# Sums and lower parts of the second layer's weight blocks on GpSimd instead of VectorE

## Chip, cores and metric

The kernel runs on one core of a Trainium2 chip. The metric is the device time of one execution in microseconds, taken as the median of the runs. Besides TensorE (PE in the profile) a core has VectorE (DVE), ScalarE (ACT), GpSimd (POOL) and SyncE (SP), each with an instruction queue of its own that is worked off in order. Nearly all transfers are issued from SP's queue.

## The reference, cut to what matters

Four batches of 512 rows and 256 columns go through two layers. Each layer normalizes the rows, computes a mixer (a recurrence with one step in the first layer, causal attention in the second) and a gated feed-forward block of width 1024 with a Walsh-Hadamard transform, and adds the product of mixer and gate to the input:

```python
xn = _layernorm(x, axis=-1)
s = _L1_attn_ref(xn, L1_attn_qkv, L1_attn_o_proj, L1_attn_gamma, L1_attn_beta)
g = _silu(_L1_ffn_ref(xn, L1_ffn_W1, L1_ffn_W2, L1_ffn_W3))
x = x + s * g

def _L1_ffn_ref(x, W1, W2, W3):
    up_gate = jnp.einsum('bsd,hd->bsh', x, W1)
    up_lin = jnp.einsum('bsd,hd->bsh', x, W3)
    hidden = jax.nn.silu(up_gate) * up_lin
    hidden = fwht(hidden)
    return jnp.einsum('bsh,dh->bsd', hidden, W2)
```

Everything is float32.

## The kernel before

**Products in two parts.** TensorE multiplies in a rounded float32 format (`F32R`). To keep float32 accuracy an operand is split into an upper part, the value rounded, and a lower part, the value minus the upper part. `split` (L59) does this: a cast on ScalarE (L61) and a subtraction on VectorE (L62). A product is three matmuls: upper by upper, upper by lower, lower by upper (`mm3`, L80). Every matmul of the kernel is recorded at L70, every split at L61 and L62, so the profile is read by tile names rather than lines.

**First layer.** `ffn` (L474) runs once per batch. For each of eight chunks `c` it makes two products of 128x512 (`f_<b>gu<c>`, three PSUM banks in turn), a silu on ScalarE (L535), the gate product on VectorE (L537, which frees the second bank), the split of the hidden tile (`f_<b>hh`, `f_<b>hl`), and, one chunk later, 24 down products of 128x256 into `f_<b>dn`.

**Work beside it.** `Beside` (L893) deals out other tasks between the chunks: the gate of the batch before (L714, L716), the mixer (L725, with `osb`, the scale `ssr` and its power on GpSimd at L740), and the norm of the next batch (`norm`, L438), which ends in a power on GpSimd (L282), the normalization (L284), and eight transposes on TensorE. The first products of a batch need the split result of these transposes, `xt`.

**The second layer's weights.** The second layer computes a 2x2 block product with seven products instead of eight; for that it needs, besides blocks of the weights, four sums of blocks. `prep_s(q)` (L327) makes them for block pair `q` of four: it loads four blocks (`sraw`, 512 KB), forms the sums `ssum` (L335 to L338, where L337 reads L335's result and L338 L337's), splits three of the blocks (128x768, after which the parts are called `sp`) and the four sums (128x1024), and stores the parts to DRAM (`s`, L347). It runs for pair 0 in the third batch of the first layer (batch 2) ahead of the next batch's norm, for pairs 1 and 2 later in that batch's tasks, and for pair 3 in batch 3. `load_s` (L350) loads the parts (`sw`, 896 KB each) for every pair of every batch of the second layer, into buffers that the first layer's weights leave. Raw blocks, sums, parts, and many other tiles share ten buffers of the tag `t4` in turn.

**Order.** In the first layer a scheduler arranges the instructions of each engine's queue from the order and the dependencies of the program; `after(...)` forces single pairs. In the second layer TensorE's order is written out by hand (`line["fixed"]`, L1089).

GpSimd runs, apart from five memsets, only the small powers at L266, L282, L402 and L740.

Of the kernel before, what the change touches and what calls it, by code (L numbers as in the profile page):

```python
# [17 lines left out]
ALU = mybir.AluOpType  # L18
# [17 lines left out]
def kernel(ctx: ExitStack, tc: tile.TileContext, a: dict, out: bass.AP):  # L36
    nc = tc.nc
# [6 lines left out]
    def t4(name, shape, dt=F32):  # L44
        return act.tile(shape, dt, tag="t4", name=name, bufs=10)
# [13 lines left out]
    def split(src, hi, lo, engine=nc.vector):  # L59

        h = nc.scalar.copy(hi, src)  # L61
        return h, engine.tensor_tensor(lo, src, hi.bitcast(F32), ALU.subtract)  # L62
# [264 lines left out]
    def prep_s(q):  # L327

        raw = t4(f"sraw{q}", [P, 4, D])
        nc.sync.dma_start(raw, a["w13_1"][q])  # L330
        yield
        sums = t4(f"ssum{q}", [P, 4, D])
        a11, a12, a22, a21 = (raw[:, i, :] for i in range(4))
        s1, s2, s3, s4 = (sums[:, i, :] for i in range(4))
        nc.vector.tensor_tensor(s1, a21, a22, ALU.add)  # L335
        nc.vector.tensor_tensor(s3, a11, a21, ALU.subtract)
        nc.vector.tensor_tensor(s2, s1, a11, ALU.subtract)  # L337
        nc.vector.tensor_tensor(s4, a12, s2, ALU.subtract)  # L338
        yield
        sdram[q] = there = [  # L340
            dram.tile([P, 7, D], F32, tag=f"s{i}", name=f"s{i}_{q}", bufs=4) for i in range(2)
        ]
        for at, n, src in ((0, 3, raw), (3, 4, sums)):
            parts = [t4(f"sp{at}_{i}_{q}", [P, n, D], F32R) for i in range(2)]
            split(src[:, :n, :], *parts)
            for i in range(2):
                nc.sync.dma_start(there[i][:, at : at + n, :], parts[i].bitcast(F32))  # L347
            yield
# [573 lines left out]
    def run(f, *args):  # L922
        return lambda: f(*args)
# [90 lines left out]
    for b in range(B):  # L1014
# [8 lines left out]
        if b + 1 < B:  # L1023
            if b:
                load_x(b + 1)
            if b == 2:
                tasks.append((prep_s(0), 4))
            tasks.append((norm(0, b + 1), NORM))
# [11 lines left out]
        if b == 2:  # L1040
            tasks += [(prep_s(1), 4), (norm(1, 0), NORM), (prep_s(2), 4)]
        if b == 3:
            atts = [Attention(0)]
            at = atts[0]
            parts = run(at.xt_half, 0), run(at.xt_half, 1), at.xt, at.scaled, at.split_sums
            tasks += [(call(f), 1) for f in parts]
            norms = {1: norm(1, 1)}
            tasks.append((prep_s(3), 4))
# [158 lines left out]
```

## Time and profile before

| what | value |
|---|---|
| median of three runs (lowest, highest) | 358.3 us (358.22, 358.42) |
| span of the profiled execution | 356.7 us |
| mean granted TensorE clock in it | 0.998 |
| VectorE busy | 287.2 us, 598 instructions |
| ScalarE busy | 197.8 us, 374 instructions |
| GpSimd busy | 20.8 us, 22 instructions |
| HBM read, written | 42.40 MB, 9.45 MB |

The span runs from the first to the last instruction of the profiled execution; the device time of a run also holds what lies around it. That execution has no device time of its own beside its span; the median is 1.6 us above the span. In the profile's lines a name such as `f_2hl<-f_2h,f_2hh` gives the tile written and the tiles read, with buffer numbers left out; in lists of groups come the count, the busy time and the mean duration of one, in a timeline the start, the duration and, in square brackets, the idle time before and what ended it. Busy time of TensorE is modelled at its ends: matmuls overlap, so a 128x512 matmul is shown with some 0.39 us though the next starts 0.23 us later.

### The profile page before, as it was taken

To read this page: it belongs to the slowest core of one execution; us is meant where nothing else is said; L and a number is where in the kernel's file an instruction comes from. 1 tells how busy PE (TensorE), PEld (TensorE's weight loads), DVE (VectorE), ACT (ScalarE), POOL (GpSimd) and SP (SyncE) were. 2 spreads that over 40 slices of the span, in tenths; PEclk is the share of its full clock that TensorE was granted. 3 is DMA by queue.
4 is the path that set the end of the run, shared out by engine and by line. 5 is a ranking of instruction groups with operands and counts; after the bars stand their busy time and mean duration, and the time that the engine had idled before them with its cause. 6 is when DMAs were issued, how large, how long until landed. Compare 5 with 4: busy or idle time off the path is not lost.

```text
span 356.7 us, 6276 instructions
## 1 busy us (share of the span) xinstructions
PE 350.9 (98%) x2477; PEld 327.5 (92%) x2477; DVE 287.2 (81%) x598; ACT 197.8 (55%) x374; POOL 20.8 (6%) x22
## 2 busy tenths in 40 slices
PE   8999999999999999999999999999999999999995
PEld 6878998888988898888999999999999999999994
DVE  6899659998579938998887957989679897678646
ACT  3666166265463425674467655586555676556443
POOL 2000110300020210100110001100011000000000
PEclk9999999999999999999999999999999999999999
DMA  6935000301044317656257145662554635445401
GB/s 208 367 98 205 2 1 2 117 0 61 0 167 163 145 38 230 257 174 191 118 208 265 36 172 209 217 201 115 206 187 168 230 158 206 143 152 186 199 2 59
DMA packets 16284, 52.25 MB, mean 146 GB/s; under 512 B 1632, under 2 KB 7936, under 8 KB 16256
## 3 DMA queue, kind: packets, MB, share of 16 engines
q1 hardware_dynamic: 15968, 51.60, 40.8%
q8 instruction: 19, 0.31, 0.4%
q10 hardware_dynamic: 288, 0.26, 0.2%
q14 instruction: 9, 0.07, 0.1%
HBM read 42.40 MB, written 9.45 MB: 145 GB/s over the span
## 4 chain that ended last, share of the span: by engine, by line
PE 98%; DVE 1%; ACT 0%; issue 0%
PE f_0dn L70 6%; PE f_1dn L70 6%; PE f_2dn L70 6%; PE f_0gu L70 6%; PE f_1gu L70 6%; PE f_2gu L70 6%; PE f_3gu L70 6%; PE f_3dn L70 6%; PE sc L70 4%; PE pv L70 4%; PE o L70 3%; PE v L70 3%; PE tq L70 3%; PE warm L70 2%; PE w2ps L70 1%; PE pt L70 1%
## 5 line engine op out<-in xcount | busy, mean ns | idle before, releaser
L70 PE MATMUL f_3gu<-xt,w 128*128 128x512 f32 x96 | 25.0, 396 | 0.0
L70 PE MATMUL f_2gu<-xt,w 128*128 128x512 f32 x96 | 24.8, 395 | 0.0
L70 PE MATMUL f_1gu<-xt,w 128*128 128x512 f32 x96 | 24.8, 395 | 0.0
L70 PE MATMUL f_0gu<-xt,w 128*128 128x512 f32 (+1 forms) x108 | 24.3, 378 | 0.0
L70 PEld LDWEIGHTS f_0gu<-xt,w 128*128 128x128 f32 x108 | 18.4, 188 | 4.5 <-issue 0.7
L70 PEld LDWEIGHTS f_1gu<-xt,w 128*128 128x128 f32 x96 | 17.0, 188 | 3.1
L70 PEld LDWEIGHTS f_2gu<-xt,w 128*128 128x128 f32 x96 | 17.0, 188 | 3.0
L70 PEld LDWEIGHTS f_3gu<-xt,w 128*128 128x128 f32 x96 | 17.0, 188 | 2.9
L61 ACT CAST f_2hh<-f_2h 128x512 fp32r<-128x512 f32 x16 | 10.0, 623 | 15.6 <-DVE f_2h L537 12.4
L70 PE MATMUL f_3dn<-w2l,f_3hh 128*128 128x256 f32 x64 | 17.7, 281 | 0.0
L70 PE MATMUL f_3dn<-w2h,f_3hh 128*128 128x256 f32 x64 | 17.7, 281 | 0.0
L70 PE MATMUL f_1dn<-w2l,f_1hh 128*128 128x256 f32 x64 | 17.7, 281 | 0.0
L70 PE MATMUL f_2dn<-w2h,f_2hh 128*128 128x256 f32 x64 | 17.7, 282 | 0.0
L70 PE MATMUL f_1dn<-w2h,f_1hh 128*128 128x256 f32 x64 | 17.6, 280 | 0.0
L70 PE MATMUL f_2dn<-w2l,f_2hh 128*128 128x256 f32 x64 | 17.6, 280 | 0.0
L70 PE MATMUL f_3dn<-w2h,f_3hl 128*128 128x256 f32 x64 | 17.0, 281 | 0.0
L70 PE MATMUL f_1dn<-w2h,f_1hl 128*128 128x256 f32 x64 | 17.0, 281 | 0.0
L70 PE MATMUL f_2dn<-w2h,f_2hl 128*128 128x256 f32 x64 | 16.7, 281 | 0.0
L61 ACT CAST f_3hh<-f_3h 128x512 fp32r<-128x512 f32 (+1 forms) x17 | 10.0, 595 | 10.2 <-DVE f_3h L537 6.0
L61 ACT CAST f_1hh<-f_1h 128x512 fp32r<-128x512 f32 x16 | 9.9, 621 | 9.7 <-DVE f_1h L537 6.6
L62 DVE TENSOR_TENSOR f_2hl<-f_2h,f_2hh 128x512 fp32r<-128x512 f32 x16 | 10.9, 684 | 4.5 <-ACT f_2hh L61 4.5
L62 DVE TENSOR_TENSOR f_3hl<-f_3h,f_3hh 128x512 fp32r<-128x512 f32 (+1 forms) x17 | 11.1, 655 | 3.7 <-ACT f_3hh L61 3.6
(487 smaller groups left out, 1147.7 us busy)
## 6 DMA issues: line engine op xcount, KB each, us to landing
sw<-s SPq DMA_DIRECT2D x32, 896.0 KB, 5.9
s<-sp SPq DMA_DIRECT2D x8, 512.0 KB, 4.2
s<-sp SPq DMA_DIRECT2D x8, 384.0 KB, 2.8
w2raw<-in_w SPq DMA_DIRECT2D x4, 512.0 KB, 5.5
sraw<-in_w SPq DMA_DIRECT2D x4, 512.0 KB, 3.5
mrb<-there SPq DMA_DIRECT2D x4, 512.0 KB, 3.8
w13raw<-in_w SPq DMA_DIRECT2D x3, 512.0 KB, 7.2
x<-in_x SPq DMA_DIRECT2D x3, 512.0 KB, 3.4
```

The source lines that it names most:

```text
L61: h = nc.scalar.copy(hi, src)
L62: return h, engine.tensor_tensor(lo, src, hi.bitcast(F32), ALU.subtract)
L70: ins = call(*args, **kwargs)
```

## The change

The four sums of `prep_s` and the subtractions of its two splits are issued on GpSimd. The casts stay on ScalarE, the transfers on SP. It applies to all four block pairs. `split` already has a parameter for the engine of the subtraction, with VectorE as the default.

```diff
         sums = t4(f"ssum{q}", [P, 4, D])
         a11, a12, a22, a21 = (raw[:, i, :] for i in range(4))
         s1, s2, s3, s4 = (sums[:, i, :] for i in range(4))
-        nc.vector.tensor_tensor(s1, a21, a22, ALU.add)
-        nc.vector.tensor_tensor(s3, a11, a21, ALU.subtract)
-        nc.vector.tensor_tensor(s2, s1, a11, ALU.subtract)
-        nc.vector.tensor_tensor(s4, a12, s2, ALU.subtract)
+        nc.gpsimd.tensor_tensor(s1, a21, a22, ALU.add)
+        nc.gpsimd.tensor_tensor(s3, a11, a21, ALU.subtract)
+        nc.gpsimd.tensor_tensor(s2, s1, a11, ALU.subtract)
+        nc.gpsimd.tensor_tensor(s4, a12, s2, ALU.subtract)
         yield
...
         for at, n, src in ((0, 3, raw), (3, 4, sums)):
             parts = [t4(f"sp{at}_{i}_{q}", [P, n, D], F32R) for i in range(2)]
-            split(src[:, :n, :], *parts)
+            split(src[:, :n, :], *parts, engine=nc.gpsimd)
             for i in range(2):
                 nc.sync.dma_start(there[i][:, at : at + n, :], parts[i].bitcast(F32))
             yield
```

Line numbers are the same in both kernels. The scheduler arranges the queues anew. In the built order of the changed kernel:

- GpSimd: pair 0's L335 to L337 and 768-column subtraction stand ahead of mixer 2's power (L740); L338 and the 1024-column subtraction follow it. Pair 1's sums and 768-column subtraction stand ahead of the two powers at L282 of batch 2 (batch 3's norm and the second layer's first norm), its last subtraction after them. Pair 2 stands ahead of mixer 3's power, and pair 3, without its last subtraction, ahead of the power of the second layer's batch 1.
- SP: the load of pair 1 stands, as before, after the stores of pair 0's first three parts; of these the store of the cast sums is now the last, where it was the store of the 768-column lower part. The load of pair 3 stands after one more weight load (`sw`, pair 1).
- TensorE: the same instructions; some groups of products change places, among them the eight transposes for batch 3, which stand after twelve more down products of batch 2.

## Prediction

> **What bounds the kernel now.** I read the page first (busy shares, the chain that ended last), then what TensorE waited for, then busy time by stretch, then the timelines of VectorE, GpSimd and TensorE between 95 and 175 us, where the change lies.
>
> ```profile
> PE 350.9 (98%) x2477; PEld 327.5 (92%) x2477; DVE 287.2 (81%) x598; ACT 197.8 (55%) x374; POOL 20.8 (6%) x22
> ...
> PE 98%; DVE 1%; ACT 0%; issue 0%
> ```
>
> TensorE is busy 98% of the span and is 98% of the chain. Its whole list of waits is one line:
>
> ```profile
> PE warm L70 <- DVE zr L941: 1.5, 1, 1.5
> ```
>
> So TensorE waits once, for the first tile at the start. The stretches confirm it (length, then busy us of PE, weight loads, DVE, ACT, POOL, with instruction counts; clock; DMA share; GB/s):
>
> ```profile
> 104.00:112.00 8.00, 8.00 (x44) 6.84 (x43) 7.70 (x19) 2.56 (x4) 1.48 (x1) 1.00 0.78 262
> 112.00:120.00 8.00, 8.00 (x48) 6.90 (x47) 8.00 (x27) 3.18 (x5) 2.55 (x2) 1.00 0.34 132
> ...
> 136.00:144.00 8.00, 8.00 (x50) 7.05 (x49) 7.04 (x13) 4.46 (x9) 0.00 (x0) 1.00 0.70 231
> ...
> 152.00:160.00 8.00, 8.00 (x44) 6.79 (x44) 8.00 (x13) 6.14 (x10) 0.00 (x0) 1.00 0.51 152
> ```
>
> TensorE is full in each, at granted clock 1.00. VectorE is full in two of them but nobody on the chain waits for it. Work taken off VectorE can therefore shorten nothing; the question is only whether something arrives late enough to open a hole in TensorE.
>
> **What is removed.** The rows of the moved work, four of each (ns min/median/max, first and last start):
>
> ```profile
> L335 DVE TENSOR_TENSOR ssum<-sraw x4: 415/418/426, 98.4 to 158.3; 128x256 f32<-128x256 f32 x4
> L338 DVE TENSOR_TENSOR ssum<-sraw,ssum x4: 412/421/426, 99.6 to 162.0; 128x256 f32<-128x256 f32 x4
> L62 DVE TENSOR_TENSOR sp<-sraw,sp x4: 917/952/953, 102.5 to 159.0; 128x768 fp32r<-128x768 f32 x4
> L62 DVE TENSOR_TENSOR sp<-ssum,sp x4: 1215/1222/1227, 103.4 to 163.7; 128x1024 fp32r<-128x1024 f32 x4
> ```
>
> Per pair of blocks VectorE loses 4 x 0.42 + 0.95 + 1.22 = 3.85 us, in all four 15.4 us. Worth on the chain: 0, by the waits above.
>
> **What is added, and its price.** GpSimd gets the same 24 instructions. The trace has no large elementwise operation on GpSimd, only 128x4 powers, so both ends are bounds. Low: VectorE's rows, 3.85 us a set. High: a fixed 1.01 us (the undisturbed power) plus two passes, one per operand, at ScalarE's pace; its casts of 768 and 1024 columns take 0.83 and 1.044 us, 0.84 ns a column. That gives 1.44 us for 256 columns, 2.29 for 768, 2.72 for 1024, a set 10.8 us. I take the middle, 0.93, 1.62 and 1.97 us, a set of 7.3 us: the power's 1.01 holds arithmetic that an addition lacks, while its 128x4 size shows that GpSimd's fixed cost is well above VectorE's 0.16 us on 128x4. A rule against the change stands in the Trainium skill, GPSIMD Engine Reference, section on performance versus the Vector engine: a two-input operation has one read port there and runs about twice as long, 4497 ns for 2048 columns. By it my estimate of a set would be 6.2 us (2.2 ns a column); no row here shows it.
>
> **GpSimd and VectorE beside each other.** The powers of one shape differ:
>
> ```profile
> 103.57 1.91 POOL L740 TENSOR_TENSOR ssr<-ssr,mhalf 128x4 f32<-128x4 f32 x1 [36.90 <-DVE ssr L739]
> 115.30 1.40 POOL L282 TENSOR_TENSOR ln_3r<-ln_3r,mhalf 128x4 f32<-128x4 f32 x1 [9.81 <-DVE ln_3r L281]
> ...
> 169.78 1.01 POOL L282 TENSOR_TENSOR ln_1r<-ln_1r,mhalf 128x4 f32<-128x4 f32 x1 [20.85 <-DVE ln_1r L281]
> ```
>
> The 1.01 one has VectorE idle beside it; the 1.91 one lies under two VectorE subtractions with both inputs in SBUF (103.40 to 105.23). I charge either engine one operation of the other per meeting: 0.69 us to a power, up to 0.93 us to a VectorE subtraction. The Trainium skill, SBUF — State Buffer, section on the two separate sides, says that the two share a port pair held for the whole instruction while the other blocks fully; the stretched powers agree. By that rule each of VectorE's two-input subtractions in these stretches could wait a whole 1024-column operation, 2.25 us by the page above, instead of 0.93.
>
> **Queues that are moved past.** In the built order of the changed kernel GpSimd's powers stand behind the new work: mixer 2's (L740) behind the first 768-column subtraction, those of batch 3's norm and of the second layer's first norm (L282) behind the three sums, the subtraction and L338 of block pair 1; second-layer batch 1's behind L338 of pair 3. VectorE waits for each power in order, and behind that wait stand the gate products (L537) that free TensorE's PSUM banks. ScalarE's casts of the sums now wait for GpSimd, with the silus behind them. On the SP queue the load of pair 1 stands behind the store of the first cast sums, and the load of pair 3 behind a weight load that was issued at 155.97.
>
> Pair 0, from times in the trace. The cast of the first three blocks ends at 101.73; subtraction to 103.35; power, stretched as before, to 105.4 (was 105.48, no change); L338 to 106.3; cast 1.04 to 107.35; store and then load of pair 1 issued at 107.75, where it was 103.96.
>
> Pair 1. A 512 KB load takes 3.5 us (median); this one, issued at 103.96, was waited for until 109.92, nearly 6. Landing is thus 111.3 to 113.7; I take 113.0. Three sums, subtraction and L338 are 5.35 us, to 118.35; the power 1.0 plus two meetings with VectorE at 0.69 less a little overlap, 120.5 (was 116.70). Then VectorE in its new order: normalization 1.37, gate product 0.6, second normalization 1.37, statistics 1.39, a subtraction 0.6, aggregates 0.5, two lower parts of xt 1.27, gate product 0.68: 128.3, in round. The PSUM bank that it frees is the one that the first product of batch 3 needs at 127.67. **Stall 0.7 us.** The transposes of batch 3 wait for the normalization too, but the new order puts 12 down products (1.42 us) ahead of them, at 121.2, and they go tile by tile as it ends at 121.9; what they lose is part of the same 0.7.
>
> The tight place before it:
>
> ```profile
> 111.61 0.65 DVE L62 TENSOR_TENSOR f_2hl<-f_2h,f_2hh 128x512 fp32r<-128x512 f32 x1
> 112.19 0.41 DVE L335 TENSOR_TENSOR ssum<-sraw 128x256 f32<-128x256 f32 x1
> ...
> 113.02 0.65 DVE L537 TENSOR_TENSOR f_2h<-f_2h,f_2gu 128x512 f32<-128x512 f32 x1
> ```
>
> TensorE takes that f_2hl at 113.24, 1.0 us after its end, and the bank behind L537 at 114.18, 0.5 us after. One meeting there (0.93), or L742 and L745 held up by L338, uses this up. **Stall 0.4 us.** These two add, since the second starts from a load that is not moved by the first.
>
> Pair 2. The data lands at 136.8 as before; sums, subtraction, L338 end at 141.15 to 141.5, the cast that took 141.53 to 142.58 stays; the silu behind it comes at 143.5 instead of 142.48, and TensorE asks for its bank near 146.3. Nothing; cover 2.2 us. Pair 3. Loaded at 156.4, landed 159.9, sums to 162.7, subtraction behind its cast to 164.6, L338 165.5, cast to 166.6 (0.2 to 0.5 late for tq's casts, score products start at 174.98), last subtraction behind the power, 170.5; its store must precede weight loads issued at 179.83. Nothing; beyond these 9 us each microsecond late is one on TensorE.
>
> **Sum.** The profiled execution has a span of 356.7 us, the runs a median of 358.3: 1.6 us lie around the span. 0.7 + 0.4 = 1.1 on the span makes 357.8, and 358.3 + 1.1 = 359.4 on the clock of the runs.
>
> **Rivals.** *Hidden after all* (not slower). If GpSimd is near VectorE's rows, pair 1's chain is 0.51 x 4 + 0.67 = 2.7 us shorter on its own and 1.2 shorter ahead of the load; the 0.7 is covered and 0.4 vanishes: 358.3. For it: no TensorE wait at all today, 2 us of cover at most places. The path holds five sums and two subtractions; 0.1 us less on each covers the 0.7, so it decides from 0.83 us a sum downward. Against: 1.01 us for a tiny power.
>
> *GpSimd dear.* At 1.44, 2.29 and 2.72 us pair 0's path to the load is 1.2 longer and pair 1's 2.7: 0.7 + 0.4 + 3.9 = 5.0; pair 2's L338 ends at 144.85, cast, two copies and silu (1.05, 1.07, 0.6) at 147.6 against 146.3, 1.3 more: 6.3, so 364.6. For it: meetings are charged once here and may repeat. Against: the power is not an addition.
>
> *Faster through order.* TensorE's order changes; a change of shape costs a little (119.91 to 120.11 where 0.12 is common). Some 0.1 us each, a handful of places: 357.9. Nothing larger, as there is no wait to remove.
>
> **How the numbers follow.** Forecast 0.48, hidden 0.25, dear 0.24, faster through order 0.03. The forecast's own range is 358.8 to 361.5. The range for all reaches from 357.9 (order) to 364.6 (high price), and the prices make both ends. About 0.2%, 0.7 us, is what a measurement of this kernel tells from no change: faster 0.03, same 0.25, slower 0.72.
>
> **What would show it.** Right: TensorE waits for VectorE or ScalarE between 112 and 130 us, about 1 us in all; GpSimd's 128x256 sums near 0.9 us; batch 3's normalization starting 3 to 4 us later; the load of pair 1 issued near 107.7. Wrong: TensorE still full from 15 to 350 us (hidden), sums over 1.4 us or VectorE's f_2hl rows doubled (dear), or a hole at 180 or 203 us, where the second layer's weights are loaded, which I price at nothing.

## The result, and the profile after

The changed kernel takes 360.28 us (median of four runs, 360.19 to 360.35), the kernel before 358.36 beside it (four runs, 358.22 to 358.53): 1.0052 times as long, with an interval of 1.0040 to 1.0064, or some 1.9 us. The profiled spans are 358.6 and 356.7 us. The forecast of 359.4 and its direction hold; the place that it names doesn't.

Busy time and chain on the page of the kernel after:

```profile
PE 351.5 (98%) x2477; PEld 327.4 (91%) x2477; DVE 284.0 (79%) x574; ACT 197.2 (55%) x374; POOL 51.3 (14%) x46
...
PE 94%; DVE 4%; issue 1%; POOL 0%; ACT 0%; DVEq 0%
```

GpSimd has 30.5 us more, 7.6 us a pair. VectorE lost 24 instructions that took 15.4 us and is only 3.2 us less busy: its other work got 12.2 us longer. VectorE now holds 4% of the chain, and TensorE waits for it at two new places (waits of TensorE: us in total, times, longest):

```profile
PE f_0gu0g L70 <- DVE f_0h L666: 0.6, 1, 0.6
PE v L70 <- DVE tql L62: 0.3, 1, 0.3
```

The stretch in which the forecast expects the loss, and two later ones (busy us of PE, weight loads, DVE, ACT, POOL):

```profile
112.00:120.00 8.00, 8.00 (x48) 7.00 (x47) 7.23 (x17) 3.18 (x5) 8.00 (x8) 1.00 0.35 137
...
170.00:176.00 6.00, 5.74 (x49) 5.53 (x49) 6.00 (x11) 3.72 (x8) 2.24 (x1) 1.00 0.45 180
176.00:182.00 6.00, 5.36 (x45) 5.16 (x45) 5.93 (x18) 1.42 (x3) 1.01 (x1) 1.00 0.00 0
```

The two later ones in the kernel before:

```profile
170.00:176.00 6.00, 6.00 (x54) 6.00 (x52) 5.13 (x12) 3.53 (x6) 0.79 (x1) 1.00 0.34 137
176.00:182.00 6.00, 6.00 (x49) 5.96 (x48) 5.37 (x19) 3.25 (x5) 1.01 (x1) 1.00 0.17 37
```

Between 112 and 120 us GpSimd is full and TensorE loses nothing. It has holes from 170 to 182 us, where the second layer begins, and there VectorE is full. The two groups of matmuls that start late, on TensorE's timeline (start, duration, idle time before and its releaser):

```profile
174.01 0.51 PE L70 MATMUL v<-wvoh,xgh 128*128 128x256 f32 x2 [0.26 <-DVE tql L62]
...
180.52 0.97 PE L70 MATMUL f_0gu0g<-tb,sw 128*128 128x256 f32 x6 [0.64 <-DVE f_0h L666]
```

Both wait for a PSUM bank that VectorE has yet to read: `v` takes a bank from the three that `tq` uses too, and `f_0gu0g` is written again after L666. The idle time shows 0.26 and 0.64 us; counted by starts the holes cost more. The products behind the first start 0.55 us later than before (`f_0gu0g` at 174.83, 174.28 before), those behind the second 1.45 (`f_0gu1g` at 181.33, 179.88 before).

What they wait for leads back along VectorE's timeline:

```profile
169.82 3.53 DVE L284 TENSOR_SCALAR xn<-x,ln_1mv,ln_1r 128x256 f32<-128x256 f32 x4 [1.13 <-POOL ln_1r L282]
173.28 0.68 DVE L62 TENSOR_TENSOR tql<-tq,tqh 128x512 fp32r<-128x512 f32 x1
...
179.79 0.67 DVE L666 TENSOR_TENSOR f_0h<-f_0gu0g,f_0h 128x512 f32<-128x512 f32 x1
```

VectorE in the kernel before:

```profile
172.17 0.41 DVE L284 TENSOR_SCALAR xn<-x,ln_1mv,ln_1r 128x256 f32<-128x256 f32 x1
...
173.09 1.06 DVE L284 TENSOR_SCALAR xn<-x,ln_1mv,ln_1r 128x256 f32<-128x256 f32 x3
...
177.45 0.66 DVE L666 TENSOR_TENSOR f_0h<-f_0gu0g,f_0h 128x512 f32<-128x512 f32 x1
```

The normalization of the second layer's batch 1 takes 3.53 us; its four operations take 1.47 in the kernel before. The two tql come at 173.28 and 174.54 (167.32 and 168.75 before), L666 at 179.79 (177.45 before). Beside the normalization lies, on GpSimd:

```profile
163.03 1.29 POOL L335 TENSOR_TENSOR ssum<-sraw 128x256 f32<-128x256 f32 x1 [13.28 <-DMA sraw<-in_w]
...
167.49 1.18 POOL L338 TENSOR_TENSOR ssum<-sraw,ssum 128x256 f32<-128x256 f32 x1
168.77 1.02 POOL L282 TENSOR_TENSOR ln_1r<-ln_1r,mhalf 128x4 f32<-128x4 f32 x1
169.83 2.41 POOL L62 TENSOR_TENSOR sp<-ssum,sp 128x1024 fp32r<-128x1024 f32 x1
```

Pair 3's last subtraction starts right behind the power that releases the normalization, so subtraction and normalization lie on the same 2.4 us. It is so late because the pair's load is. SP's timeline, first of the kernel before, then of the one after:

```profile
148.44 0.42 SPq L330 DMA_DIRECT2D sraw<-in_w  x1
155.97 0.32 SPq L355 DMA_DIRECT2D sw<-s  x1
```

```profile
148.10 9.19 SPq L355 DMA_DIRECT2D sw<-s  x2
157.38 0.38 SPq L330 DMA_DIRECT2D sraw<-in_w  x1
```

Before, the load goes out at 148.44, ahead of a weight load (`sw`, pair 1) that waits for a buffer; after, it stands behind that weight load and goes out at 157.38.

Where the time went can be read from the starts of four matmuls on TensorE's timeline, counted from the first product of the first layer (`f_0gu`, at 7.84 us before and 7.61 after): A is the first product of batch 3 (`f_3gu`), B the first of the second layer (`f_0gu0g`), C that layer's second group (`f_0gu1g`), D its last batch (`f_3gu0g`). Each row gives the us by which it is later than in the kernel before (119.83, 162.89, 172.04 and 300.28 us); the kernels below the first are those of the next section, some of them with their loss elsewhere.

| profiled kernel | A | B | C | D |
|---|---|---|---|---|
| after | 0.17 | 0.26 | 1.68 | 1.71 |
| pair 3 on VectorE, load late | 0.28 | 1.27 | 1.28 | 1.30 |
| pair 3 alone on GpSimd, load first | 0.03 | 0.52 | 0.52 | 0.53 |
| last subtraction on VectorE, load late | 0.16 | 0.25 | 0.25 | 0.53 |
| last subtraction after the normalization, load late | 0.22 | 0.30 | 0.60 | 0.63 |
| last subtraction in four, load late | 0.16 | 0.24 | 1.18 | 1.25 |
| all on GpSimd, load first | 0.16 | 0.24 | 0.23 | 0.23 |
| last subtraction on VectorE, load first | 0.23 | 0.30 | 0.29 | 0.33 |
| pair 3 on VectorE, load first | 0.38 | 0.46 | 0.45 | 0.47 |
| pair 1 alone on GpSimd, load first | 2.50 | 2.55 | 2.54 | 2.55 |

For the changed kernel: the first product 0.23 earlier, 0.26 lost up to B, 1.42 from B to C, 0.03 up to D, and 0.41 more behind D (48.55 us before, 48.96 after), 1.9 in all. The start of the first product (7.50 to 7.97 us) and the stretch behind D (48.5 to 49.1) vary among these profiles, and why was not found. The 0.41 lies behind VectorE's last operation, which ends at 354.12 us before and at 355.61 after, 1.49 apart where D is 1.48; only the last transfers are left there. What is lost between the first product and D is taken here as the change's.

### The profile page after: what moved, and what is told of

The parts are those of the page before. It is cut to its first block, busy times and chain, and to the rows that moved or that the text cites. A ratio compares the mean times of both kernels' runs of the same rounds, so it can differ in the third digit from the quotient of the medians.

```text
span 358.6 us, 6297 instructions
## 1 busy us (share of the span) xinstructions
PE 351.5 (98%) x2477; PEld 327.4 (91%) x2477; DVE 284.0 (79%) x574; ACT 197.2 (55%) x374; POOL 51.3 (14%) x46
## 4 chain that ended last, share of the span: by engine, by line
PE 94%; DVE 4%; issue 1%; POOL 0%; ACT 0%; DVEq 0%
PE f_0dn L70 6%; PE f_1dn L70 6%; PE f_2dn L70 6%; PE f_0gu L70 6%; PE f_3gu L70 6%; PE f_1gu L70 6%; PE f_2gu L70 6%; PE f_3dn L70 5%; PE pv L70 4%; PE sc L70 4%; PE o L70 3%; PE v L70 3%; PE tq L70 2%; PE warm L70 2%; PE w2ps L70 1%; PE pt L70 1%
## 5 line engine op out<-in xcount | busy, mean ns | idle before, releaser
L62 DVE TENSOR_TENSOR f_2hl<-f_2h,f_2hh 128x512 fp32r<-128x512 f32 x16 | 12.8, 802 | 5.3 <-ACT f_2hh L61 5.1
L62 DVE TENSOR_TENSOR f_3hl<-f_3h,f_3hh 128x512 fp32r<-128x512 f32 (+1 forms) x17 | 13.0, 769 | 4.7 <-ACT f_3hh L61 4.5
```

## The experiments

Two theories stood at the start. T1: the loss is pair 3's, at the layer boundary, since its load lands at 163 us. R1, the step on record: it is pair 1's, in the norm stage of batch 3.

**Pair 3 back on VectorE, load late.**

```diff
-        nc.gpsimd.tensor_tensor(s1, a21, a22, ALU.add)
+        (nc.vector if q == 3 else nc.gpsimd).tensor_tensor(s1, a21, a22, ALU.add)
...
-            split(src[:, :n, :], *parts, engine=nc.gpsimd)
+            split(src[:, :n, :], *parts, engine=nc.vector if q == 3 else nc.gpsimd)
```

> Sums and subtractions of pairs 0, 1 and 2 on GpSimd as in the changed kernel, those of pair 3 back on VectorE. Its load still stands behind the first weight load of pair 1 on SP's queue, as in the changed kernel. Theory T1 (the 1.9 us are lost at the layer boundary, because pair 3's six GpSimd operations, started by a load that lands at 163 us, push the casts of tqh from 166.7 and 168.1 to 169.7 and 171 and hold up the normalization until 173.3): without these operations the waits of TensorE on tql and on f_0h are gone; 358.4 to 358.8 us, 0.3 of it being what pairs 0 to 2 cost. Rival R1 (the step on record: pairs 0 to 2, in the norm stages of batches 2 and 3, cost 1 us or more): 359.4 to 360.3. Rival R2 (the load's lateness alone, whichever engine does the sums): VectorE has 4.5 us of work to do from 163 on, ahead of the same normalization; 359.5 to 360.3, with the hole at 174 us still there.

Measured 359.99 us, ratio 1.0042 (1.0029 to 1.0054). T1 as stated misses. The time fits R1 and R2 alike; by the table only 0.28 us is lost up to A, where R1 puts its 1 us or more, so what is left is R2, the lateness of the load whatever the engine. The hole that R2 names at 174 isn't there. TensorE's waits in this kernel have this line instead, and by the table 1.0 us is lost between A and B:

```profile
PE f_3dn L70 <- DVE f_3hl L62: 0.6, 1, 0.6
```

VectorE does the pair's sums and subtractions between 163.3 and 169.2 us, and an f_3hl behind them starts at 169.94 (168.09 before).

**Pair 3 alone on GpSimd.** Here the scheduler leaves the load ahead of the weight load.

```diff
-        nc.gpsimd.tensor_tensor(s1, a21, a22, ALU.add)
+        (nc.gpsimd if q == 3 else nc.vector).tensor_tensor(s1, a21, a22, ALU.add)
...
-            split(src[:, :n, :], *parts, engine=nc.gpsimd)
+            split(src[:, :n, :], *parts, engine=nc.gpsimd if q == 3 else nc.vector)
```

> The mirror: only pair 3's sums and subtractions on GpSimd, those of pairs 0 to 2 on VectorE as before. By its order of instructions pair 3's load stands ahead of pair 1's weight load on SP's queue, as in the kernel before, so it should be issued near 148 and land near 153 us. T1 in its narrow form (lateness of the load, then GpSimd's pace): six operations from 153 on end at about 162, ahead of the normalization at 168, and nothing is lost: 358.3 to 358.7. R1 (pairs 0 to 2 cost it): 358.3 to 358.5 too, so this run parts T1 from R1 only together with the run in which pair 3 alone is back on VectorE. R2' (GpSimd's pace and its hold on VectorE at pair 3, whenever the load lands): 359.7 to 360.3, with the normalization still near 3.5 us.

358.88 us, 1.0016 (1.0007 to 1.0025), 0.2 above T1's range and well below R2'. With the load issued at 148.61 GpSimd can do all of pair 3 at 0.6 us. By the timelines most of that is one meeting: L784, a product of two SBUF inputs, takes 2.34 us beside the 768-column subtraction (0.68 before), and behind the late L537 that follows, TensorE starts its products at 161.50 after 0.24 us of idle time.

**The last subtraction of pair 3 on VectorE, load late.**

```diff
-            split(src[:, :n, :], *parts, engine=nc.gpsimd)
+            split(src[:, :n, :], *parts, engine=nc.vector if q == 3 and at else nc.gpsimd)
```

> The changed kernel, but pair 3's last subtraction (128x1024) on VectorE, where it stands right ahead of the normalization and takes 1.2 us instead of lying beside it for 2.4. T1: the casts of tqh stay as late as they are (169.7 and 171.1 us); the normalization takes 1.4 us instead of 3.5 and ends near 172.4 instead of 173.3, so that about half of the loss goes: 359.2 to 359.7. R3 (the hold of GpSimd's subtraction on the normalization is all of the loss at the boundary): 358.6 to 358.9. R4 (the late casts are all of it): 360.1 to 360.4, unchanged.

359.65 us, 1.0037 (1.0025 to 1.0049), as T1 said; the profiled execution, at 359.26 the fastest of its runs, has nothing left of the boundary's loss (C in the table), though the two casts of tqh are nearly as late as in the changed kernel (they start at 169.28, there at 169.66). So R4, the late casts alone, falls.

**Pair 3's load first, all on GpSimd.**

```diff
-        nc.sync.dma_start(raw, a["w13_1"][q])
+        first["sload"] = nc.sync.dma_start(raw, a["w13_1"][q])
...
-            nc.sync.dma_start(parts[i].bitcast(F32), sdram[q][i])
+            with after(first["sload"] if n == 1 else None):
+                nc.sync.dma_start(parts[i].bitcast(F32), sdram[q][i])
```

> The changed kernel with one order changed: on SP's queue the load of pair 3 stands ahead of pair 1's first weight load, which waits 8.5 us for TensorE, instead of behind it. All of the operations stay on GpSimd. T1: the load is issued at 148 to 150 us instead of 157.4, lands by 155, GpSimd is through with the pair by 165, the casts of tqh are back at about 167 and 168.5, the normalization is at its 1.4 us, and no wait of TensorE on tql or f_0h is left: 358.4 to 358.8. R2' (GpSimd's pace and hold at pair 3 cost it, whenever the load lands): 359.7 to 360.3. R1 (pairs 0 to 2): 360 to 360.3, since they are as in the changed kernel.

359.09 us, 1.0019 (1.0010 to 1.0028), an interval that lies below the changed kernel's. One place in SP's queue is worth about 1.2 us of the 1.9. The expected 358.8 was missed by 0.3. GpSimd isn't through by 165 either: the first subtraction waits 4.97 us for its cast on ScalarE, and the last one still meets VectorE. Timelines of GpSimd and VectorE in this kernel:

```profile
167.89 2.62 POOL L62 TENSOR_TENSOR sp<-ssum,sp 128x1024 fp32r<-128x1024 f32 x1 [3.66 <-ACT sp L61]
```

```profile
168.44 2.10 DVE L281 TENSOR_SCALAR ln_1r<-ln_1mv 128x4 f32<-128x4 f32 x1
```

An addition of 128x4 elements takes 2.10 us (0.17 before) and ends with the subtraction beside it. TensorE doesn't see it.

**The last subtraction behind the normalization, load late.** A 128x4 operation that reads the normalization's last output holds GpSimd up.

```diff
+            if q == 3 and at:
+                nc.scalar.copy(parts[0], src)
+                nc.sync.dma_start(there[0][:, at:, :], parts[0].bitcast(F32))
+                first["rest"] = src, parts, there
+                return
...
                 next(norms[1])
+                src, parts, there = first["rest"]
+                with after(first["scaled"]):
+                    nc.gpsimd.tensor_tensor(parts[1][:, 0, :4], xns[1, 1][:, 3, -4:], mhalf, ALU.add)
+                    nc.gpsimd.tensor_tensor(parts[1], src, parts[0].bitcast(F32), ALU.subtract)
+                nc.sync.dma_start(there[1][:, 3:, :], parts[1].bitcast(F32))
```

> The changed kernel with pair 3's load late as in it, and all operations on GpSimd, but the last subtraction (128x1024) made to wait for the normalization: a 128x4 operation on GpSimd that reads the normalization's last output is put ahead of it. So the subtraction costs GpSimd the same and can no longer lie beside the normalization. T2 (the late load sets off the loss, and what TensorE sees of it is the hold of GpSimd's subtraction on VectorE): the normalization is back near 1.4 us, f_0h and tql come 1.5 to 2 us earlier, the two holes of TensorE at 174 and 180.5 us are gone; 359.2 to 359.8, as with the subtraction on VectorE (359.65). R4 (the late casts alone): 360.1 to 360.4. R5 (the subtraction holds up whatever VectorE does next, so the loss only moves): 359.9 to 360.4, with another VectorE operation near 2 to 3 us at 173 to 176.

359.15 us, 1.0018 (1.0010 to 1.0027). VectorE's timeline:

```profile
170.01 0.74 DVE L284 TENSOR_SCALAR xn<-x,ln_1mv,ln_1r 128x256 f32<-128x256 f32 x2 [1.13 <-POOL ln_1r L282]
...
171.27 0.73 DVE L284 TENSOR_SCALAR xn<-x,ln_1mv,ln_1r 128x256 f32<-128x256 f32 x2
...
173.49 1.87 DVE L719 TENSOR_TENSOR g_3g<-g_3g,xn 128x512 f32<-128x512 f32 x1
```

The normalization is back at 1.47 us. The hold has moved on, as R5 expected, to the gate's product (L714 of the kernel before, 0.69 us), but there nobody on TensorE waits: B to C loses 0.3 instead of 1.42. With the load and the casts as late as in the changed kernel, this is the run that shows the hold on the normalization to be what TensorE feels. VectorE's order differs a little here (the first tql stands inside the normalization, at 170.66 us); with the last subtraction on VectorE both tql stand behind the whole normalization, as in the changed kernel, and the boundary's loss is gone there too.

**Load first and the last subtraction on VectorE.** The order of the loads as above, and

```diff
-            split(src[:, :n, :], *parts, engine=nc.gpsimd)
+            split(src[:, :n, :], *parts, engine=nc.vector if q == 3 and at else nc.gpsimd)
```

> Pair 3's load ahead of pair 1's weight load, and pair 3's last subtraction on VectorE. With the load first and everything on GpSimd the time was 359.09, and its trace still shows a hold: ln_1r's addition of 128x4 elements on VectorE took 2.10 us beside the last subtraction (0.16 in the kernel before). T2: that hold goes too, 358.7 to 359.0. If holds that TensorE doesn't see cost nothing: 359.0 to 359.2, as without the step.

359.02 us, 1.0016 (1.0007 to 1.0025), the same as without the second edit: L281 is back at 0.17 us, and that hold, which nobody on TensorE waited for, cost nothing that these runs can tell.

**Load first and pair 3 on VectorE.** The order of the loads as above, the four sums likewise, and

```diff
-            split(src[:, :n, :], *parts, engine=nc.gpsimd)
+            split(src[:, :n, :], *parts, engine=nc.vector if q == 3 else nc.gpsimd)
```

> Pairs 0 to 2 on GpSimd, pair 3 on VectorE, and pair 3's load ahead of pair 1's weight load. Its twin with the load behind took 359.99. T2 (the load's place in SP's queue is the larger part of the loss, on whichever engine the sums are): 358.5 to 359.0, that is 1.0 to 1.5 below the twin; what is left over 358.3 is the price of pairs 0 to 2, 0.2 to 0.7. Rival (VectorE's order around pair 3, changed by the scheduler, is what cost the twin its time): 359.7 to 360.1.

358.90 us, 1.0013 (1.0004 to 1.0022), below its twin with the load behind (1.0029 to 1.0054). The load's place counts on either engine, about 1.0 us here by the two ratios.

**The last subtraction in four pieces, load late.**

```diff
-            split(src[:, :n, :], *parts, engine=nc.gpsimd)
+            nc.scalar.copy(parts[0], src[:, :n, :])
+            for k in range(n) if q == 3 and at else (slice(0, n),):
+                nc.gpsimd.tensor_tensor(parts[1][:, k, :], src[:, k, :], parts[0][:, k, :].bitcast(F32), ALU.subtract)
```

> The changed kernel with pair 3's last subtraction on GpSimd cut into four of 128x256; the load stays late. One of 128x1024 took 2.41 us and the normalization beside it 3.53. T2 (VectorE is held until the GpSimd operation at hand ends, so that the length of one operation sets the hold): in the probe with additions of 128x256 the normalization took 0.73 us each beside them, so about 2.9 us in all here, a gain of 0.5: 359.5 to 360.0. R5 (GpSimd's total time is what is taken from VectorE; cutting it helps nothing, and each operation's start adds some): 360.2 to 360.6.

359.51 us, 1.0032 (1.0019 to 1.0045): T2's size, though the interval still touches the changed kernel's. VectorE's timeline has the normalization at 3.14 us, and B to C loses 0.94:

```profile
169.61 3.14 DVE L284 TENSOR_SCALAR xn<-x,ln_1mv,ln_1r 128x256 f32<-128x256 f32 x4 [1.13 <-POOL ln_1r L282]
```

The hole at `v` is gone, the one at `f_0gu0g` still shows 0.6 us. GpSimd's four pieces take 2.98 us in place of 2.41, so R5's extra is there too, and is smaller than the gain.

**Pair 1 alone on GpSimd, load first.**

```diff
+        (nc.gpsimd if q == 1 else nc.vector).tensor_tensor(s1, a21, a22, ALU.add)
...
+            split(src[:, :n, :], *parts, engine=nc.gpsimd if q == 1 else nc.vector)
```

> Pair 1 alone on GpSimd, with pair 3's load ahead of pair 1's weight load; pairs 0, 2 and 3 on VectorE as before. The step on record puts 1.1 us of loss (0.7 and 0.4) on pair 1 in the norm stage of batch 3: 359.4 us then. What the runs up to now leave for pairs 0 to 2 together is about 0.5 (358.9 with them on GpSimd and the load first): if it is all pair 1's, 358.7 to 359.0; if pairs 0 and 2 have a share or it is the order of TensorE's work, 358.4 to 358.7.

360.83 us, 1.0069 (1.0055 to 1.0083): all three guesses miss, and this kernel is slower than the whole change. TensorE's new waits:

```profile
PE xt_3tp L70 <- DVE xn L284: 0.8, 1, 0.8
PE f_2dn L70 <- DVE f_2hl L62: 0.5, 1, 0.5
PE f_2gu L70 <- DVE f_2h L538: 0.2, 1, 0.2
```

Here TensorE loses at both places on record: at the tight place (`f_2hl`), and in the norm stage, where more is lost at the transposes than at the bank behind the gate product (L538, the L537 of the kernel before) that the forecast named. Batch 3's normalization takes 3.45 us beside pair 1's last subtraction, and 2.5 us are gone by A. The changed kernel has the same 3.45 us:

```profile
118.11 3.45 DVE L284 TENSOR_SCALAR xn<-x,ln_3mv,ln_3r 128x256 f32<-128x256 f32 x4
```

and loses 0.17. By the timelines the difference is TensorE's order; no run changes that order alone. With pair 1 alone on GpSimd the scheduler puts the first transposes at 117.7 us, in the changed kernel all eight at 120.92, after more products of batch 2.

**Pairs 0, 2 and 3 on GpSimd, pair 1 on VectorE, load first.** A slip in the edit also changed the line that chooses the engine of the second layer's copies (L645, L651, L654), so that three of four groups copy on VectorE instead of one:

```diff
-            copy = nc.vector.tensor_copy if q == 1 else nc.scalar.copy
+            copy = nc.vector.tensor_copy if q in (0, 2, 3) else nc.scalar.copy
```

> Pairs 0, 2 and 3 on GpSimd, pair 1 on VectorE, pair 3's load first. With pair 1 on GpSimd too the time was 359.09. If what is left there is pair 1's, through the normalization of batch 3 that its last subtraction holds up (3.45 us for 1.37): that normalization is back at 1.4 us and the time at 358.3 to 358.7. If it is not (the order of TensorE's products, or what GpSimd's other operations hold up): 358.9 to 359.3.

379.95 us, 1.0615, which says nothing on pair 1: the loss lies in the second layer, where the copies are (D comes 23.35 us later than in the kernel before). Up to it the profile can be read: A and B are at 119.77 and 162.90 us from the first product, 0.06 earlier and 0.01 later than in the kernel before. So the 0.26 us that the changed kernel loses in the first layer goes when pair 1 leaves GpSimd, by this one profile.

**Which operations hold each other up.** To the kernel before, 40 operations of 128x256 are added on GpSimd in the second layer, first with two inputs, then with one.

```diff
             nc.gpsimd.tensor_tensor(rs, rs, mhalf[:, :n], ALU.pow)
+            if name == "ln1_2":
+                scratch = wp.tile([P, D], F32, name="scratch")
+                nc.gpsimd.memset(scratch, 0.0)
+                nc.gpsimd.tensor_tensor(scratch[:, :n], rs, mhalf[:, :n], ALU.add)
+                for _ in range(40):
+                    nc.gpsimd.tensor_tensor(scratch, scratch, scratch, ALU.add)
```

> The kernel before, with 40 additions of 128x256 elements added on GpSimd (scratch plus scratch, in a chain, some 0.73 us each undisturbed) that start with the second layer's third normalization, near 220 us, and run beside whatever VectorE does for the next 30 to 50 us. It measures which forms of VectorE's work are held up. From the trace of the changed kernel: the one-input normalization (L284) 0.7 to 0.9 us each instead of 0.41, the 128x512 operations on two inputs of SBUF (L670, L62) 0.8 to 2.2 instead of 0.69; those with an input in PSUM (L663, L666, L645) 0.69 unchanged, statistics (L261, L277) 0.41 unchanged; the additions themselves 0.73 to 1.3. If the hold is only between operations of two SBUF inputs, the normalization stays at 0.41. Time: 359 to 366, since TensorE is held up where VectorE is late.

```diff
-                    nc.gpsimd.tensor_tensor(scratch, scratch, scratch, ALU.add)
+                    nc.gpsimd.tensor_scalar(scratch, scratch, 1.0, None, ALU.mult)
```

> The probe again with 40 operations of one input on GpSimd (multiply by 1.0, 128x256, in place) instead of additions. If an operation of GpSimd holds VectorE whatever its inputs: the normalization near 0.73 us each and several 128x512 operations at 0.8 to 1.1, as beside the additions, 361 us or so. If it takes two inputs on GpSimd: the normalization at 0.41, all 128x512 operations at 0.65 to 0.69, and 358.3 to 358.8 us.

361.3 and 359.09 us (one run each; 358.53 and 358.31 before). VectorE's timeline beside the additions, and then beside the operations of one input:

```profile
220.49 2.47 DVE L290 TENSOR_SCALAR xn<-x,ln_2mv,ln_2r 128x256 f32<-128x256 f32 x4 [1.12 <-POOL ln_2r L282]
...
236.18 0.68 DVE L722 TENSOR_TENSOR x<-x,g_0g 128x512 f32<-128x512 f32 x1
...
252.24 1.10 DVE L676 TENSOR_TENSOR f_1h<-f_1h,f_1v 128x512 f32<-128x512 f32 x1
```

```profile
220.60 1.82 DVE L290 TENSOR_SCALAR xn<-x,ln_2mv,ln_2r 128x256 f32<-128x256 f32 x4 [1.12 <-POOL ln_2r L282]
```

Beside additions the normalization (L284 of the kernel before, four in 1.37 us there) takes 0.62 us an operation on average, 0.73 the last two, and the products of two SBUF inputs between 0.68 (L722, not held) and 1.10 (L676). Beside operations of one input it takes 0.46, and the 128x512 rows up to 257 us stay at 0.65 to 0.88. So the answer lies between the two that were expected: an input less on GpSimd leaves a little of the hold.

## Why the prediction was right, and where it was wrong

The direction was right, and 360.28 lies inside the forecast's own range of 358.8 to 361.5, but for another reason than the one given: of its 1.1 us, laid at the norm stage of batch 3, only 0.26 came up to B, and 1.42 came at a place that it priced at nothing. That the time still fell inside the range is luck. Of its own signs of being right, the load of pair 1 came true (107.13 us), and the sums, at 0.73 to 1.29 us, lie around the 0.9 named. But TensorE doesn't wait between 112 and 130 us, and batch 3's normalization starts 1.35 us later (118.11 for 116.76), not 3 to 4.

**VectorE's relief is worth nothing.** Right; 15.4 us left it and the kernel is slower.

**GpSimd's price.** Right in the total. The rows of the moved work (ns min/median/max):

```profile
L335 POOL TENSOR_TENSOR ssum<-sraw x4: 737/1015/1292, 84.3 to 163.0; 128x256 f32<-128x256 f32 x4
L338 POOL TENSOR_TENSOR ssum<-sraw,ssum x4: 737/1186/1195, 104.9 to 167.5; 128x256 f32<-128x256 f32 x4
L62 POOL TENSOR_TENSOR sp<-sraw,sp x4: 1834/1847/1857, 101.5 to 165.7; 128x768 fp32r<-128x768 f32 x4
L62 POOL TENSOR_TENSOR sp<-ssum,sp x4: 2380/2409/2577, 106.8 to 169.8; 128x1024 fp32r<-128x1024 f32 x4
```

Undisturbed a sum takes 0.73 to 0.74, a set 4 x 0.74 + 1.85 + 2.41 = 7.2 us against the forecast's 7.3; with what VectorE adds it is 7.6. The forecast set the sums too dear and the subtractions too cheap, and the two cancel. Its reason for a high fixed cost, the power's 1.01 us on 128x4, doesn't hold: an addition of 128x4 elements on GpSimd took 0.20 us, both in the run with the last subtraction behind the normalization and in the one with 40 additions. The rule that it cites from the Trainium skill, GPSIMD Engine Reference, section on performance versus the Vector engine (about twice VectorE's time), fits: 1.85 to 0.95, 2.41 to 1.22, 0.74 to 0.42. The estimate of 6.2 us a set, worked out from its figure at 2.2 ns a column, is 1.0 too low: each operation took 0.16 to 0.18 us more than that.

**The norm stage of batch 3: 0.7 + 0.4 us.** The mechanism is real, the size wrong: 0.26 us up to B. Its times came out early: pair 1's load at 107.13 (forecast 107.75), its data at 111.19 (113.0), the power's end at 117.80 (120.5). The normalization ends at 121.56, against the forecast's 121.9, but by another sum: the power is 2.7 us earlier than forecast, and the normalization, taken at 1.37, lasts 3.45. The tight place at 114 us, on VectorE's timeline:

```profile
111.51 1.07 DVE L62 TENSOR_TENSOR f_2hl<-f_2h,f_2hh 128x512 fp32r<-128x512 f32 x1
...
112.72 0.65 DVE L537 TENSOR_TENSOR f_2h<-f_2h,f_2gu 128x512 f32<-128x512 f32 x1
...
114.05 2.17 DVE L62 TENSOR_TENSOR f_2hl<-f_2h,f_2hh 128x512 fp32r<-128x512 f32 x1
```

The first f_2hl meets GpSimd once (0.42 longer), and L537 is still no later than before (0.07 us earlier, counted from the first product), since L335 and L336 no longer stand between them. The removed work paid for the meeting; the forecast counted only the meeting. The second f_2hl is held too (2.17 us, 0.68 before) and TensorE has no hole there. The transposes' later place on TensorE, which the forecast did count, covered most of the rest: the eight start 0.10 to 0.11 us apart but for two steps, to 121.62 and 121.79, around the end of the normalization at 121.57. Pair 1 alone on GpSimd, with another order of TensorE's work, lost 2.5 us.

**Pair 2: nothing.** Right. L338 ends at 142.30 (forecast 141.15 to 141.5) and the silu starts at 144.24 (143.5); the cover held.

**Pair 3: "Nothing; beyond these 9 us each microsecond late is one on TensorE."** This is the step that failed: 1.42 us from B to C. The queue order was seen, and the load went out 1.0 us later than forecast (157.38 for 156.4). The flight was taken at the median 3.5 us, and was 5.65, behind a weight load issued 0.4 us earlier (5.6 too where the load goes first, from 148.51 to 154.14); so L338 ends at 168.67 instead of 165.5 and the last subtraction at 172.24 instead of 170.5. That alone would have left cover for the store. What was missing is the other reader of the time: the step measured the chain against its own store only, and not against VectorE's normalization, which stands behind the same power and which GpSimd's last subtraction then holds up. Take away the hold (subtraction after the normalization) or the lateness (load first) and most of the loss goes, with all of the work still on GpSimd. The forecast's own list of what would prove it wrong has a hole at 180 us, but one left by late weight loads; the hole at 180.5 is VectorE's.

**One meeting, one operation of 0.69 to 0.93 us.** The sort of work was too narrow: the charge was laid on VectorE's subtractions with two SBUF inputs and never on the normalization, which reads one (beside its per-row scalars). And it was too small: held beside a 1024-column subtraction, VectorE loses about 2 us (3.53 against 1.47, L281's 2.10 against 0.17), and f_2hl, a subtraction of the kind that was charged, lost 1.49 beside a 768-column one (2.17 against 0.68). The Trainium skill, SBUF — State Buffer, section on the two separate sides, which the forecast weighed and put aside at 2.25 us, has the right size. Its condition, VectorE operations with two SBUF inputs or in a two-port mode, doesn't name these two by their inputs; whether they run in such a mode no run here shows.

**The rivals.** *Hidden* set its condition at 0.83 us a sum; undisturbed the sums met it at 0.74, the 768-column subtractions came out 0.23 dearer than forecast, and the norm stage was nearly hidden. It failed for the boundary above all. *Dear* falls with the rows above. *Faster through order*: where order mattered it cost (SP) or merely covered (TensorE).

**What stays open.** With the load first the ratios leave 0.13 to 0.19% (0.5 to 0.7 us), and the markers place 0.2 to 0.5 of it, up to B. The rest isn't placed. That the first layer's share is pair 1's rests on one profile and on the steps of the transposes. No version here beats the kernel before, nor is one in sight, since TensorE had no wait to give back.

## What to carry to other kernels

When work moves to another engine, follow its DMA issues through a queue that is worked off in order: a load that slips behind one instruction with a long wait is late by that wait, and here its place was worth about 1.2 us of the 1.9. Check a late chain not only against its own consumer but against everything on the neighbour engine that will run in the same microseconds, above all against what is released by the same event as its last operation. A meeting of two engines can cost nearly the whole of the longer operation (here 2.06 of 2.41 us), so look at its order first: putting the long one behind the urgent one took 1.1 us off the time. Cutting it into four took off 0.8 by the medians, with intervals that still touch.

## What the hardware showed that was not expected

The normalization and L281, operations of VectorE with a single SBUF tensor beside per-row scalars or a constant, are held up by GpSimd's two-input operations, and a small size doesn't spare them: 128x4 elements took 2.10 us beside a 1024-column subtraction, 0.17 without. Not every operation with a single SBUF tensor is held: the statistics of L277 stayed at 1.40 us for four beside a sum and the 768-column subtraction (165.10 to 166.50 us in the changed kernel). Nor was L537, which has an input in PSUM; it stayed at 0.65 to 0.69 us in both kernels. GpSimd's operations are stretched in turn, by 0.44 to 0.55 us a sum (0.74 to 1.18, and 1.29).

In a meeting of two operations with SBUF inputs either of the two can be the one that is held. Beside the run of additions the product L722 starts at 236.18 us, 0.03 ahead of an addition, and takes its 0.68; that addition takes 1.12, where the one at 233.12 takes 0.61. The product L676 starts at 252.24, 0.39 behind an addition, and takes 1.10. These two fit the reading that the earlier one goes first. Recorded starts don't settle every case: the L722 at 228.52 starts 0.20 behind an addition and isn't held (the addition takes 1.35), and the normalization at 169.82 in the changed kernel starts 0.01 ahead of the subtraction and is held.
